# Two graph layers' aggregates as seven products of 128-column adjacency sums, with VectorE adding plus terms from PSUM

## The chip, the cores and the metric

The kernel runs on one core of one Trainium2 chip. The metric is the device time of one execution in microseconds (us). The core's engines are TensorE (PE, with its weight loads as PEld), VectorE (DVE), ScalarE (ACT), GpSimd (POOL) and SyncE (SP), which issues the transfers. Each engine has its own instruction queue and works through it in order; semaphores tie the queues together.

## The reference

There are 64 graphs of 256 nodes and 512 features, all in float32. Two layers follow each other:

```python
h = relu(adj @ (x @ W1) + b1)
h = relu(adj @ (h @ W2) + b2)
x = layernorm(x + adj @ (h @ W3) + b3)

q, k = split(x @ Wqk); v = x @ Wv
agg = adj @ (k * mask[:, :, None])
w = inv_scale * mask * sum(q * agg, axis=-1)
x = layernorm(x + softmax(w)[:, :, None] * v)
```

The inputs' mask is all ones, but the kernel applies it.

## The kernel before

Graphs are taken in 32 pairs (G = 2). All tiles have 128 partitions; 512 float columns fill one of the eight PSUM banks.

Most products use the same scheme, `seven`: a 2x2 block product made of seven block products instead of eight, from sums of the blocks of either operand. It runs the products in the order 1, 7, 6, 2, 5, 4, 3 in three PSUM banks, copies three partial results to SBUF tiles named `tmp` (ScalarE), and ends each of the four result blocks with a function that its caller gives (`c11`, `c12`, `c21`, `c22`). Where the caller gives `plus`, GpSimd adds that term to the copied tile.

For each pair of graphs:

- `support` (L304) computes h @ W with `seven`, once for each of the three layers. Its left operands are the blocks of the activations and their sums, made by `a_sums` (four sums, all on GpSimd); its right operands are weight blocks and sums made once.
- `aggregate` (L326) computes adj @ support for layers 1 and 2, without `seven`: four PSUM banks, one for each 128 output features, with two 256-column matmuls for each graph. ScalarE applies bias and ReLU out of PSUM into `hT` (L329), and GpSimd makes the next `a_sums`.
- `adj_times` (L362) computes adj @ something with `seven` and sums of adj (`adj_sums`, GpSimd) and of the other operand (`t_sums`, four sums on GpSimd): once for layer 3, once for the attention's gather of the normalized `xm`.
- `back` adds x, makes the statistics (BN_STATS, L439 and L441), `xm` on ScalarE (L456), the normalized `r` (L458) and its transposes (L484) on VectorE, which go through DRAM to become `x1T`.
- `attention` (L542) multiplies by W products held in DRAM as 28 slices, `mv`, read through a ring of seven SBUF tiles (`ring`): each use issues the fetch for the seventh use after it. It nests `seven` twice: 28 inner steps, of which the last 14 alternate between two matmuls and one.
- `finish` does softmax over the nodes, the last sum, layer norm and the store.

These parts are Python generators. Steps of F (`front`: supports and aggregates of one pair), S (`sums`), B (`back`) and G, M (gather and attention of the pair before), and E (`finish` of the pair before that) are interleaved by four strings written out by hand: START for the first pair, ORDER for most, LAST and END for the last ones. One letter runs one generator up to its next `yield`. The strings so fix the order of instructions on every engine.

Of the kernel before, what the change touches and what calls it, by code (L numbers as in the profile page):

```python
# [14 lines left out]
P = 128  # L15
# [5 lines left out]
def gcn_then_graph_attention(ctx: ExitStack, tc: tile.TileContext, xT, xN, adjT, mask, W1, b1, W2, b2, W3, b3,  # L21
                             WqT, WkT, Wv, out):

# [7 lines left out]
    KEYS = ("T1", "T2", "T3", "T4")  # L47

# [12 lines left out]
    def tmp():  # L61
        return pool.tile([P, D], FP, name="tmp", bufs=6)
# [3 lines left out]

    def padd(o, a, b, op=OP.add):
        nc.gpsimd.tensor_tensor(o, a, b, op=op)  # L68
# [18 lines left out]
    def load_x(i):  # L87
        t = pool.tile([P, G, NH, D], FP, name="x", tag="x", bufs=1)
        nc.sync.dma_start(t, xN[i].rearrange("p (g h f) -> p g h f", g=G, h=NH))
        return t  # L90


    def b_steps(B, Ts, eng):

        sub = OP.subtract
        for o, a, b in ((2, B[3], B[1]), (0, B[1], B[0]), (1, B[3], Ts[0]), (3, B[2], Ts[1])):
            eng.tensor_tensor(Ts[o], a, b, op=sub)
            yield

    def b_sums(B, Ts, eng):  # L100
        for _ in b_steps(B, Ts, eng):
            pass

    def shaped(shape):
        t = tmp()
        if len(shape) == 2:
            return t
        return t[:, :shape[1] * shape[2]].rearrange("p (a b) -> p a b", a=shape[1])

    def seven(mm, shape, c11, c12, c21, c22, plus=None):  # L110

        x = bank(shape)
        mm(1, x, True)
        t1 = shaped(shape)
        nc.scalar.copy(t1, x)  # L118
        if plus is not None:
            padd(t1, t1, plus[0])  # L120
        yield
        v = bank(shape)
        mm(7, v, True)
        yield
        mm(6, x, False)
        u = shaped(shape)
        nc.scalar.copy(u, x)  # L127
        yield
        y = bank(shape)
        mm(2, y, True)  # L130
        t7 = shaped(shape)
        nc.scalar.copy(t7, v)  # L132
        if plus is not None:
            padd(t7, t7, plus[2])
            padd(u, u, plus[1])
        c11(y, t1)
        yield
        mm(5, x, False)
        c22(x, t7)
        yield  # L140
        mm(4, v, False)
        c21(v, u)
        yield
        mm(3, x, False)
        c12(x)
        yield

# [44 lines left out]
    mask_t = const.tile([P, NH, NPAIR * G], FP, name="mask_t")  # L192
    mask_s = const.tile([P, NH, NPAIR * G], FP, name="mask_s")
    eps = const.tile([P, 1], FP, name="eps")
    nc.vector.memset(eps, EPS)

    def prepare():

        for n, w in ((2, W2), (3, W3)):
            begin, end = load_w(w, n)  # L200
            begin()
            yield from end()
        aTs[1] = load_adj(1)
        nc.sync.dma_start(b3b, b3.partition_broadcast(P))
        nc.sync.dma_start(mask_t, mask.rearrange("p (h b) -> p h b", h=NH))
        yield
        nc.vector.tensor_scalar(mask_s, mask_t, ISCALE, None, op0=OP.mult)
        yield from make_m()
# [66 lines left out]
    def a_sums(blk, eng=nc.gpsimd):  # L275

        S = [pool.tile([P, 2, G, P], FP, name="S", tag="S", bufs=8) for _ in range(4)]
        sub = OP.subtract  # L280

        def first():
            eng.tensor_tensor(S[2], blk(0, 0), blk(1, 0), op=sub)  # L283

        def rest():
            eng.tensor_tensor(S[0], blk(1, 0), blk(1, 1), op=OP.add)  # L286
            eng.tensor_tensor(S[1], S[0], blk(0, 0), op=sub)  # L287

        def last():
            eng.tensor_tensor(S[3], blk(0, 1), S[1], op=sub)  # L290
        return {1: blk(0, 0), 2: blk(0, 1), 4: blk(1, 1), 5: S[0], 6: S[1], 7: S[2], 3: S[3]}, first, rest, last

# [4 lines left out]
    def support(src, w, last=None):  # L297

        C = [[pool.tile([P, G, HD], FP, name="sup", tag="sup", bufs=7) for _ in range(2)] for _ in range(2)]

        def mm(n, ps, first):
            for g in range(G):
                for c in range(2):
# [3 lines left out]
        steps = seven(mm, (P, G, HD), lambda y, t: add(C[0][0], y, t), lambda x: nc.scalar.copy(C[0][1], x),  # L307
                      lambda v, t: add(C[1][0], v, t), lambda v, t: add(C[1][1], v, t))
# [7 lines left out]

    def aggregate(C, aT, b):


        hT = [pool.tile([P, 2, G, N], FP, name="hT", tag="act", bufs=2) for _ in range(2)]  # L320
        src, first, rest, last = a_sums(blocks(hT))
        for c in range(DC):
            ps = bank()
            for g in range(G):
                for k in range(NH):
                    nc.tensor.matmul(ps[:, g], lhsT=C[k][c // 2][:, g, (c % 2) * P:(c % 2 + 1) * P],  # L326
                                     rhs=aT[:, k, g], start=(g == 0 and k == 0), stop=(g == G - 1 and k == NH - 1),
                                     skip_group_check=True)
            nc.scalar.activation(hT[c // 2][:, c % 2], ps, AF.Relu, bias=b[:, c:c + 1])  # L329
            if c == 1:  # L330
                first()
            if c == 3:
                rest()
            yield
        return src, last

    def adj_sums(aT, put):
        S = pool.tile([P, 4, G, P], FP, name="aS", bufs=1)
        blk = lambda i, k: aT[:, k, :, i * P:(i + 1) * P]
        sub = OP.subtract  # L340
        padd(S[:, 0], blk(1, 0), blk(1, 1))
        yield
        padd(S[:, 1], S[:, 0], blk(0, 0), sub)
        yield
        padd(S[:, 2], blk(0, 0), blk(1, 0), sub)
        yield
        padd(S[:, 3], blk(0, 1), S[:, 1], sub)
        put["aS"] = {1: blk(0, 0), 2: blk(0, 1), 4: blk(1, 1), 5: S[:, 0], 6: S[:, 1], 7: S[:, 2], 3: S[:, 3]}

    def t_sums(B):  # L350
        T = pool.tile([P, 4, G, HD], FP, name="T", tag="T", bufs=1)
        Ts = [T[:, k] for k in range(4)]
        b_sums((B[0][0], B[0][1], B[1][0], B[1][1]), Ts, nc.gpsimd)
        return Ts

    def adj_times(aS, B, Ts, c11, c12, c21, c22, plus=None):

        mov = {1: B[0][0], 2: B[1][0], 3: B[1][1], 4: Ts[3], 5: Ts[0], 6: Ts[1], 7: Ts[2]}
# [17 lines left out]
    def softmax_rows(w, gs):  # L376
# [7 lines left out]
        e = small.tile([n, N], FP, name="e", bufs=1)  # L384
# [5 lines left out]
        return e  # L390

    def softmax_cols(sm, gs):
        n = len(gs)
        ps = bank((P, NH, n))
        for h in range(NH):
            nc.tensor.transpose(ps[:, h, :], sm[:, h * P:(h + 1) * P], ident[:n, :n])  # L396
# [5 lines left out]
    def front(i, hT, src, aT, put):  # L402
        C = yield from support(src, wl[1])
        if i + 1 < NPAIR:
            put["xT"] = load_xT(i + 1)
        src, last = yield from aggregate(C, aT, bcol[0])
        C = yield from support(src, wl[2], last)
        src, last = yield from aggregate(C, aT, bcol[1])
        put["x"] = load_x(i)
        return (yield from support(src, wl[3], last))  # L410

    def sums(i, aT, put):

        fs = [lambda: None] * 3
        if i + 1 < NPAIR:
            put["S"], *fs = a_sums(blocks(put["xT"], True))
# [4 lines left out]
        for g in range(G):  # L421
            for h in range(NH):
                padd(x[:, g, h, :], x[:, g, h, :], b3b)
                yield
        yield from adj_sums(aT, put)

    def back(i, C, aS, x, end, put):
        Ts = t_sums(C)
# [13 lines left out]
        yield from adj_times(aS, C, Ts, lambda y, t: add(rb(0, 0), y, t), lambda x: block(rb(0, 1), x, xb(0, 1), 0),  # L442
# [5 lines left out]
        b = i * G  # L448
        mrs = small.tile([P, NH, G], FP, name="mrs")
        nc.vector.tensor_tensor(mrs, rs, mask_t[:, :, b:b + G], op=OP.mult)  # L450
        mnb = small.tile([P, NH, G], FP, name="mnb")
        nc.vector.tensor_tensor(mnb, nb, mask_t[:, :, b:b + G], op=OP.mult)
# [9 lines left out]
        if end:  # L462
# [6 lines left out]
            Ts = t_sums(xmb)  # L469
# [7 lines left out]
        else:  # L477
# [15 lines left out]
            Ts = t_sums(xmb)  # L493
# [4 lines left out]
        def gather():  # L498
            steps = adj_times(aS, xmb, Ts, lambda y, t: add(gb(0, 0), y, t), lambda x: nc.scalar.copy(gb(0, 1), x),
# [9 lines left out]
        put["M"] = attention(i, x1b, w, r, put)  # L509

    def attention(i, x1b, w, r, put):
# [42 lines left out]
        flat = lambda R: R.rearrange("p g j f -> p g (j f)")  # L554

        def score(R, h, g):
            t = put["gt"][:, h, g, :]
            b = i * G + g
            nc.vector.scalar_tensor_tensor(t, R[:, g].rearrange("p j f -> p (j f)"), mask_s[:, h, b:b + 1], t,  # L559
                                           op0=OP.mult, op1=OP.mult, accum_out=w[:, h, g:g + 1])  # L560

        def results(g):
# [6 lines left out]
            put[g] = r, v, w  # L569
# [21 lines left out]
    def finish(i, prev, gs=range(G)):  # L591
# [3 lines left out]
        sm = softmax_rows(w, gs)  # L595
        yield
        s = softmax_cols(sm, gs)
# [16 lines left out]
        for k, g in enumerate(gs):  # L614
            for h in range(NH):
# [5 lines left out]


    ORDER = ("BFEFFFEBFBEFBBBFBBFBBFFFBFBESBEFBBGFFGEFEEGEGFFEFESFFGMMGSFEMGMMFMMMMMMMMMMMMMMMMMFM"
             "MMMMMSFMMMSSMMSMSSFMFSMFMMEMSMMFM")
    START = ("FBBFBFFFBBFBBBFBBFBBBBFBFFBBBBBBFBBFBBBBBBBBFFFFBBFBBBBBBFFBBSBFFBFBBSFBBBFFSBBBFSBB"
             "BBSBFBSBFBSSSSBSBBBSBBB")
    LAST = ("BFEFFFEBFBEFBBBFBBFBBFFFBFBESBEFBBGFFGEFEEGEGFFEFESFFGMMGSFEMGMMFMMMMMMMMMMMMMMMMMFM"
            "MMMMMSFMMMSSMMSMSSFMFSMFMMEMSMMFM")
    END = ("EEBEBEBEEBBBEEEBBBEEBBBBBBGMGMGBGMMBMEMMMMMGGMMMBMMMMGMMMMMMMMMMMMMMMMMMXMXMMMMXMMYM"
           "XMXXMXMYMYYYXXYYMMXXMYXYYYY")  # L630
# [16 lines left out]
    xS, *fs = a_sums(blocks(xTs, True))  # L647
    for f in fs:
        f()
    for i in range(NPAIR + 1):  # L650
        gens, put, done = {}, {}, {}
        if i < NPAIR:
            gens["F"] = front(i, xTs, xS, aTs[i], put)
            gens["S"] = sums(i, aTs[i], put)
# [18 lines left out]
        if i < NPAIR:  # L673
            state = (res["F"], put["aS"], put["x"])
            xTs, xS = put.get("xT"), put.get("S")
# [35 lines left out]
```

## Time and profile before

| | |
|---|---|
| Median of 3 runs | 2777.42 us (2775.81 to 2778.24) |
| Profiled execution, span (the page has no other time of it) | 2778.9 us |
| Granted TensorE clock, mean | 0.994 of full speed |
| Transfers | 403 MB, mean 145 GB/s |
| Idle time of L542's matmuls before `ring` landed | 13.1 us |

A line of the profile names an engine, an operation, the tiles that it writes and reads, how often it ran, and its durations. "Idle before" is the time that the engine was not busy just before such an instruction, with what ended it. TensorE's records: a float32 matmul leaves two.

### The profile page before, as it was taken

What the parts mean: (1) busy time and instruction counts of PE and PEld (TensorE: products, weight loads), DVE (VectorE), ACT (ScalarE), POOL (GpSimd) and SP (SyncE); (2) the same over time, 40 slices, a digit from 0 to 9 for tenths busy, and PEclk for the clock granted to TensorE, in tenths of its full rate; (3) what the DMA queues carried; (4) which work ended last, traced back from release to release, by engine and by line L of the source; (5) the groups of instructions that cost most, each with busy time, mean ns of one, the idle gap of its engine ahead of it and who ended that gap; (6) DMA issues with size and microseconds to landing.
All of it is one profiled execution on the core that took longest, in us unless ns stands there. A gap on an engine that the chain in (4) does not pass through costs nothing.

```text
span 2778.9 us, 37024 instructions
## 1 busy us (share of the span) xinstructions
PE 2731.4 (98%) x12688; PEld 2377.9 (86%) x12688; DVE 1723.4 (62%) x2900; ACT 1143.7 (41%) x1890; POOL 1795.9 (65%) x1446
## 2 busy tenths in 40 slices
PE   9999999999999999999999999999999999999996
PEld 8888888888888888888888888888888888888875
DVE  4566565665566665656666666655566655666666
ACT  3334344434444433444334444334443334443434
POOL 3666765676756666656667666767566676667663
PEclk9999999999999999999999999999999999999997
DMA  6444554344554345543445543455444455434442
GB/s 223 153 122 131 163 174 136 113 146 150 162 166 130 118 139 169 161 148 125 134 139 161 171 134 116 139 161 161 154 126 127 139 161 173 137 112 145 139 153 97
DMA packets 197752, 403.45 MB, mean 145 GB/s; under 512 B 20160, under 2 KB 57408, under 8 KB 189504
## 3 DMA queue, kind: packets, MB, share of 16 engines
q1 hardware_dynamic: 197568, 401.10, 45.8%
q8 instruction: 103, 1.69, 0.3%
q14 instruction: 81, 0.66, 0.1%
HBM read 328.54 MB, written 72.48 MB: 144 GB/s over the span
## 4 chain that ended last, share of the span: by engine, by line
PE 93%; DMA 3%; DVE 2%; issue 1%; POOL 1%; ACT 0%; SPq 0%; POOLq 0%; ACTq 0%; DVEq 0%
PE ps L304 41%; PE ps L542 22%; PE ps L326 16%; PE ps L362 14%; DMA ring<-mv 3%; PE ps L246 1%; DVE v L600 0%; DVE gt L559 0%; PE ps L381 0%; PE ps L396 0%; DMA xT<-in_xT 0%; DVE R L65 0%; POOL S L286 0%; POOL tmp L68 0%; DVE st L607 0%
## 5 line engine op out<-in xcount | busy, mean ns | idle before, releaser
L304 PE MATMUL ps<-w_T,S 128*128 128x256 f32 x2304 | 539.7, 379 | 3.8 <-POOL S L287 2.8
L304 PEld LDWEIGHTS ps<-w_T,S 128*128 128x128 f32 x2304 | 435.1, 190 | 63.9 <-POOL S L287 4.0
L326 PE MATMUL ps<-aT,sup 128*128 128x256 f32 x2048 | 457.7, 379 | 0.0
L65 DVE TENSOR_TENSOR R<-ps,tmp 128x512 f32<-128x512 f32 (+1 forms) x384 | 230.5, 622 | 365.5 <-PE ps L542 350.3
L542 PE MATMUL ps<-ring,I 128*128 128x256 f32 x1792 | 428.5, 381 | 13.3 <-DMA ring<-mv 13.1
L326 PEld LDWEIGHTS ps<-aT,sup 128*128 128x128 f32 x2048 | 389.0, 190 | 52.8
L283 POOL TENSOR_TENSOR S<-hT 128x512 f32<-128x512 f32 x64 | 81.7, 1277 | 492.1 <-ACT hT L329 492.1
L542 PEld LDWEIGHTS ps<-ring,I 128*128 128x128 f32 x1792 | 339.7, 190 | 64.7 <-issue 15.1
L127 ACT COPY tmp<-ps 128x512 f32<-128x512 f32 (+1 forms) x288 | 158.0, 560 | 446.7 <-PE ps L542 183.8
L65 DVE TENSOR_TENSOR sup<-ps,tmp 128x512 f32<-128x512 f32 x288 | 197.4, 686 | 211.6 <-PE ps L304 211.6
L542 PE MATMUL ps<-ring,Z 128*128 128x256 f32 x1344 | 321.6, 379 | 0.0
L68 POOL TENSOR_TENSOR tmp<-tmp,R 128x512 f32<-128x512 f32 (+1 forms) x192 | 213.1, 1137 | 160.2 <-DVE R L579 141.2
L542 PEld LDWEIGHTS ps<-ring,Z 128*128 128x128 f32 x1344 | 255.4, 190 | 34.7
L307 ACT COPY sup<-ps 128x512 f32<-128x512 f32 x96 | 56.2, 585 | 457.1 <-PE ps L304 303.6
L68 POOL TENSOR_TENSOR I<-Z 128x384 f32<-128x384 f32 (+1 forms) x128 | 177.7, 1409 | 100.6 <-DVE Z L523 97.1
L304 PE MATMUL ps<-w,hT 128*128 128x256 f32 x1024 | 241.9, 379 | 0.0
L118 ACT COPY tmp<-ps 128x512 f32<-128x512 f32 (+1 forms) x288 | 158.8, 563 | 172.1 <-PE ps L304 86.0
L304 PEld LDWEIGHTS ps<-w,hT 128*128 128x128 f32 x1024 | 194.6, 190 | 26.4
L329 ACT ACTIVATE hT<-ps,b 128x512 f32<-128x512 f32 x256 | 171.3, 681 | 98.6 <-PE ps L326 96.9
L68 POOL TENSOR_TENSOR tmp<-tmp,x 128x512 f32<-128x512 f32 x96 | 120.5, 1270 | 128.7 <-ACT tmp L132 128.4
L65 DVE TENSOR_TENSOR gt<-ps,tmp 128x512 f32<-128x512 f32 x96 | 65.4, 682 | 222.6 <-PE ps L362 222.6
L68 POOL TENSOR_TENSOR x<-x,b3b 128x512 f32<-128x512 f32 x128 | 202.3, 1600 | 0.0
(111 smaller groups left out, 4755.0 us busy)
## 6 DMA issues: line engine op xcount, KB each, us to landing
ring<-mv SPq DMA_DIRECT2D x672, 256.0 KB, 3.5
x<-in_xN SPq DMA_DIRECT2D x32, 1024.0 KB, 6.0
out<-v SPq DMA_DIRECT2D x64, 512.0 KB, 2.7
xT<-in_xT SPq DMA_DIRECT2D x31, 1024.0 KB, 4.8
via<-tr SPq DMA_DIRECT2D x31, 1024.0 KB, 4.3
x1T<-via SPq DMA_DIRECT2D x124, 256.0 KB, 4.7
ring<-mv SPq DMA_DIRECT2D x224, 128.0 KB, 2.9
aT<-in_adjT SPq DMA_DIRECT2D x32, 512.0 KB, 3.5
```

The lines of the kernel that those rows point to most:

```text
L65: nc.vector.tensor_tensor(o, a, b, op=OP.add)
L68: nc.gpsimd.tensor_tensor(o, a, b, op=op)
L118: nc.scalar.copy(t1, x)
L127: nc.scalar.copy(u, x)
L246: nc.tensor.matmul(pt[:, j * P:(j + 1) * P], lhsT=wq[:, d, f * P:(f + 1) * P], rhs=wk[:, d, j * P:(j + 1) * P], start=(d == 0 and j == 0), ...
L283: eng.tensor_tensor(S[2], blk(0, 0), blk(1, 0), op=sub)
L304: nc.tensor.matmul(ps[:, g], lhsT=src[n][:, c, g], rhs=w[n][:, c], start=(first and g == 0 and c == 0), stop=(g == G - 1 and c == 1), skip ...
L307: steps = seven(mm, (P, G, HD), lambda y, t: add(C[0][0], y, t), lambda x: nc.scalar.copy(C[0][1], x), lambda v, t: add(C[1][0], v, t), la ...
L326: nc.tensor.matmul(ps[:, g], lhsT=C[k][c // 2][:, g, (c % 2) * P:(c % 2 + 1) * P], rhs=aT[:, k, g], start=(g == 0 and k == 0), stop=(g == ...
L329: nc.scalar.activation(hT[c // 2][:, c % 2], ps, AF.Relu, bias=b[:, c:c + 1])
L362: nc.tensor.matmul(ps[:, g], lhsT=aS[n][:, g], rhs=mov[n][:, g], start=(first and g == 0), stop=(g == G - 1), skip_group_check=True)
L542: nc.tensor.matmul(ps[:, k], lhsT=left[n](place[o]), rhs=wt[:, k], start=(first and k == 0), stop=(k == len(outer) - 1), skip_group_check= ...
```

## The change

The aggregates of layers 1 and 2 use `seven` too. Their right operands are the 128-column blocks of adj and their three sums, which `adj_sums` now makes one pair ahead (one sum is written in place). Their left operands are blocks of the support and sums of them: `support` makes these in its last step, two from PSUM on VectorE and two by `unit`. The result blocks are added into `hT`, and ScalarE applies bias and ReLU in place, in two calls a block.

`seven` no longer copies by ScalarE where a plus term is given: VectorE adds the term straight from PSUM into `tmp`. Layer 3's `t_sums` is gone, as the support has the sums. `a_sums` and `adj_sums` write one of their sums in place, so that they need three tiles. A list, ON_DVE, says which sums VectorE makes; the others stay on GpSimd. The mask is loaded for each pair, and its scale is applied in `back`; the softmax tile is allocated once, and its transposes became plain matmuls. All four order strings are new; M, B, E, G and S have as many steps as before in each, and F has 35 in place of 29.

```diff
+    ON_DVE = ('a3', 'a5', 'a6', 'a7', 'c1T6', 'c2T4', 'c2T6', 'h13', 'h15', 'h16', 'h25', 'h26', 'h27', 'x3', 'x5', 'x6', 'x7')
+    def unit(name, o, a, b, op=OP.add):
+        (nc.vector if name in ON_DVE else nc.gpsimd).tensor_tensor(o, a, b, op=op)
 def seven(mm, shape, c11, c12, c21, c22, plus=None):
+        def out(ps, k):
+            t = shaped(shape)
+            if plus is None:
+                nc.scalar.copy(t, ps)
+            else:
+                add(t, ps, plus[k])
+            return t
-        t1 = shaped(shape)
-        nc.scalar.copy(t1, x)
-        if plus is not None:
-            padd(t1, t1, plus[0])
+        t1 = out(x, 0)
...
 def support(src, w, who, last=None):
-        C = [[pool.tile([P, G, HD], FP, name="sup", tag="sup", bufs=7) for _ in range(2)] for _ in range(2)]
+        sup = lambda: pool.tile([P, G, HD], FP, name="sup", tag="sup", bufs=SUP)
+        C = {k: sup() for k in (1, 3, 2, 5, 7)}
...
+        def c12(x):
+            sub(C[7], C[3], x)
+            sub(C[5], x, C[1])
+            C[6], C[4] = sup(), sup()
+            unit(who + "T6", C[6], C[3], C[5], OP.subtract)
+            unit(who + "T4", C[4], C[2], C[6], OP.subtract)
...
 def aggregate(C, aS, b, who):
-        for c in range(DC):
-            ps = bank()
-            for g in range(G):
-                for k in range(NH):
-                    nc.tensor.matmul(ps[:, g], lhsT=C[k][c // 2][:, g, (c % 2) * P:(c % 2 + 1) * P],
-                                     rhs=aT[:, k, g], start=(g == 0 and k == 0), stop=(g == G - 1 and k == NH - 1),
-            nc.scalar.activation(hT[c // 2][:, c % 2], ps, AF.Relu, bias=b[:, c:c + 1])
+        def relu(i, j, ps=None):
+            o = blk(i, j)
+            for c in range(2):
+                nc.scalar.activation(o[:, c], (o if ps is None else ps)[:, c], AF.Relu, bias=b[:, 2 * j + c:2 * j + c + 1])
+        def block(i, j, a, t):
+            add(blk(i, j), a, t)
+            relu(i, j)
+        def mm(n, ps, first):
+            for c in range(2):
+                for g in range(G):
+                    nc.tensor.matmul(ps[:, c, g], lhsT=C[n][:, g, c * P:(c + 1) * P], rhs=aS[n][:, g],
+                                     start=(first and c == 0 and g == 0), stop=(c == 1 and g == G - 1),
+        for k, _ in enumerate(seven(mm, (P, 2, G, P), lambda y, t: block(0, 0, y, t), lambda x: relu(0, 1, x),
+                                    lambda v, t: block(1, 0, v, t), lambda v, t: block(1, 1, v, t))):
+            if k == 5:
+                first()
+            if k == 6:
+                rest()
...
 def t_sums(B):
-        b_sums((B[0][0], B[0][1], B[1][0], B[1][1]), Ts, nc.gpsimd)
+        for n, o, a, b in (("x7", 2, B[3], B[1]), ("x5", 0, B[1], B[0]), ("x6", 1, B[3], Ts[0]), ("x4", 3, B[2], Ts[1])):
+            unit(n, Ts[o], a, b, OP.subtract)
...
 def back(i, C, aS, x, mask, end, put):
-        Ts = t_sums(C)
...
-    ORDER = ("BFEFFFEBFBEFBBBFBBFBBFFFBFBESBEFBBGFFGEFEEGEGFFEFESFFGMMGSFEMGMMFMMMMMMMMMMMMMMMMMFM"
-             "MMMMMSFMMMSSMMSMSSFMFSMFMMEMSMMFM")
+    ORDER = ("BBFFEFBFFEBFBFFBFFFFFBEFBFBBBFBFBBFBEGEFFGGGGFFMMGFGFMMMFFMFMMEMMSMEMMEEEFFMMESMSSEM"
+             "SFMFMFSMFFSMFMSMMMMMMEMMMSMSMSMMMMMMMMM")
...
```

## The prediction

> **What bounds the kernel now.** I read the busy line first, then the chain of work that ended last, to see whether another engine sets the pace.
>
> ```profile
> PE 2731.4 (98%) x12688; PEld 2377.9 (86%) x12688; DVE 1723.4 (62%) x2900; ACT 1143.7 (41%) x1890; POOL 1795.9 (65%) x1446
> PE 93%; DMA 3%; DVE 2%; issue 1%; POOL 1%; ACT 0%; SPq 0%; POOLq 0%; ACTq 0%; DVEq 0%
> PE ps L304 41%; PE ps L542 22%; PE ps L326 16%; PE ps L362 14%; DMA ring<-mv 3%; PE ps L246 1%; DVE v L600 0%; DVE gt L559 0%; PE ps L381 0%; PE ps L396 0%; DMA xT<-in_xT 0%; DVE R L65 0%; POOL S L286 0%; POOL tmp L68 0%; DVE st L607 0%
> ```
>
> TensorE is the bound: 47.5 us of the 2778.9 us span are not its work, and nothing else carries over 3% of the chain. Fewer matmul microseconds shorten the kernel as long as TensorE is fed. L326 is the part that the change rewrites. A pair takes 84.15 us from one softmax transpose to the next where no wait for the ring falls into it (mean of all about 84.7).
>
> Next, the critical chain in order of time, for the price of a matmul of either width (start, us, what, number of records; a float matmul leaves two records).
>
> ```profile
> 23.06 14.29 PE ps L246 x128
> 265.05 6.91 PE ps L326 x32
> ```
>
> L246 streams 128 columns, 111.6 ns a record, 0.2233 us a matmul. L326 streams 256, 215.9 ns a record, 0.4318 us a matmul. Both load a new 128x128 weight each time.
>
> Then single lines, with shortest, median and longest duration, for VectorE's prices.
>
> ```profile
> L65 DVE TENSOR_TENSOR sup<-ps,tmp x288: 673/690/693, 16.3 to 2700.1; 128x512 f32<-128x512 f32 x144
> L523 DVE TENSOR_TENSOR Z<-Z x64: 691/1226/1781, 125.2 to 2732.5; 128x512 f32<-128x512 f32 x64
> ```
>
> An addition from PSUM takes 0.69 us whatever else runs. One of two SBUF tiles takes 0.69 us as well, but up to 1.78 us while GpSimd works. Back to back they overlap by 0.085 us, so each holds VectorE 0.605 us, or 0.725 us if the next needs its result.
>
> Last, VectorE's timeline of one steady pair, where layer 3's sums end and the attention's input is normalized.
>
> ```profile
> 1028.07 0.69 DVE L65 TENSOR_TENSOR r<-ps,x 128x512 f32<-128x512 f32 x1 [0.26 <-PE ps L362]
> 1028.79 1.29 DVE L439 BATCH_NORM_STATS2 st<-r 128x6 f32<-128x512 f32 x2
> 1030.00 0.30 DVE L441 BATCH_NORM_AGGREGATE mvt<-st 128x2 f32<-128x6 f32 x2
> 1030.66 0.18 DVE L371 RECIPROCAL rs<-sd 128x4 f32<-128x4 f32 x1 [0.36 <-ACT sd L369]
> ...
> 1031.07 0.16 DVE L452 TENSOR_TENSOR mnb<-nb,mask_t 128x4 f32<-128x4 f32 x1
> 1032.44 0.55 DVE L458 TENSOR_SCALAR r<-r,rs,nb 128x512 f32<-128x512 f32 x1 [1.21 <-ACT xm L456]
> 1033.02 1.07 DVE L484 STREAM_TRANSPOSE tr<-r 128x256 f32<-128x256 f32 x2
> 1033.95 1.37 DVE L458 TENSOR_SCALAR r<-r,rs,nb 128x512 f32<-128x512 f32 x1
> ```
>
> This is the chain that I price below: today the T sums at its end are GpSimd's.
>
> **The aggregates.** A layer has 16 matmuls of 256 columns (6.91 us); after the change 28 of 128: 28 x 0.2233 = 6.25 us. That is 0.66 us a layer, 1.32 a pair, and over 64 layers **-42.1 us**, all on TensorE.
>
> A rule speaks against this. "TensorE: Matmul & The Clock Gate" in the Trainium skill, section "Back-to-back issue gap", gives 81 ns for a sustained matmul of 128 columns with its weight load and 131 ns for 512. A straight line between makes 256 columns about 98 ns, an estimate; 28 narrow ones would then cost 1.45 times the 16 wide ones, +6.2 us a pair or about +199 us in all. L246's row contradicts it for this data type, so I use the row.
>
> **VectorE's load.** From the instruction lists: 576 additions of 512 columns from PSUM come to VectorE (192 write hT, 192 make sup, 192 add plus terms), 96 of 256 columns, 512 of SBUF tiles of 512 columns, 128 of 256. At 0.605, 0.33, 0.66 and 0.34 us that is 348 + 32 + 338 + 44 = 762 us. GpSimd loses more than half its work (1796 to about 800 us), which lets VectorE's SBUF work go faster: the 128 score operations (L559) average 1.43 us against a shortest of about 0.74, so -80, and some -50 elsewhere. VectorE ends near 2350 us, 85%. It is no bound in total, but its queue is long, and its order decides when TensorE gets its operands. ScalarE has two shorter ReLU calls a block but loses the copies ahead of plus terms; it stays near 42%.
>
> **The new wait.** In the order after the change I looked for each product whose operand now comes from VectorE and counted TensorE's work before it. One hand-off comes short: the attention's gather (adj_times on xm). Its product 7 needs T's x7, made on VectorE behind everything in the timeline above and, by ON_DVE, behind layer 1's sums h15, h16 and h13 of the next pair (h17 stays on GpSimd). From the end of layer 3's last product, TensorE has until then: the aggregate's product 3 (4 x 0.2233), supports 1, 7, 6, 2 (16 x 0.4318), the gather's product 1 (0.86), supports 5 and 4 (3.45): **12.12 us**. VectorE meanwhile: 0.20 until r<-ps,x starts, 2.23 until the aggregates of statistics end (1028.07 to 1030.30), then new in between one st<-v (0.60 less 0.08 of overlap), h15 and h16 (0.725 + 0.605): 4.28. Reciprocal to mnb 0.57, ScalarE's xm 0.93 (the median gap there), four groups of L458 and two transposes at 1.51 without GpSimd (1032.44 to 1033.95): 11.82. h13 0.605, x7 0.69 and 0.04 to TensorE: **13.16 us**. TensorE waits 1.04 us. Product 6 needs x5 and x6, 1.33 us after x7, and has 0.86 of cover: 0.47 more. So 1.5 us a pair in 31 pairs, **+46 us**. It eats the whole saving. Behind the late x7 VectorE holds sup additions of support 2, 5 and 4; these have at least 3 us of cover. Bounds: 0.7 us a pair if gaps overlap better (+22), 2.2 if h15, h16 or L458 meet GpSimd (L458's second row shows 1.37 for 0.55; +68). I take 1.5: GpSimd's only sum there, h17 (1.27 us), should end before VectorE's SBUF work begins.
>
> **What is relieved.** Layer 3's T sums leave GpSimd's serial queue and are made with the support; of the 0.4 us that a pair is longer than its matmuls (193 x 0.4318 + 0.43 for the softmax), half lies at support 3's wait at the end of the pair, for its GpSimd sum: 0.2 x 31 = **-6** (0 to -6). The ring costs 13.1 us today, in 13 pairs, where the 1 MB load of x is queued on SP between fetches. After the change x, the small mask load (32 more issues) and the two output stores are issued where the next seven fetches have about 14 us before use. But support products no longer lie between the small ring products: six fetches a pair must land within 3.89 us of the use before (nine matmuls). They land in 3.5 us (256 KB) or 2.9 us (128 KB) in the median, plus 0.2 to issue. I take 0.3 us a pair, 9 instead of 13: **-4** (-13 to +15).
>
> **Ends.** Order END starts the last pair's layer 3 before the softmax, where TensorE now waits 2.1 and 3.5 us, and needs no GpSimd T sums: **-8** (-12 to 0). At the start VectorE makes the first x and adj sums beside weight sums: **+3** (0 to +7). The hoisted softmax buffer, mask scaling and wider tile counts move no wait that I can find: 0.
>
> **Sum** against the profiled span 2778.9 (median of the runs 2777.4, 1.5 less): -42 + 46 - 6 - 4 - 8 + 3 = **-11**, or 2768 of span, 2766 as a run. What a measurement of this kernel can tell is about 0.2%, 5.6 us.
>
> **Rivals.**
> *VectorE's chain is longer (slower).* One mechanism: the SBUF operations between the statistics and x7 collide with GpSimd, or VectorE enters the chain late because it is dense from the scores on. Each 0.1 us is 3 us. Above 1.9 us a pair the sign turns; at 2.7 it is +26, 2803. For: L458 and Z<-Z collide today. Against: GpSimd does less than half. Chance 0.24.
> *The ring becomes the bound.* 0.8 us a pair at the small products, 384 KB in 1.3 us or about 300 GB/s, above any slice of the page (223): +16 against my sum, 2782, about no change. Chance 0.12.
> *The hand-off is covered.* If x7 is at most 0.7 us late: 24 better, 2742. For: the pieces overlap by 0.08 to 0.15 us each, which I may undercount. Chance 0.14.
> *The narrow matmuls do not pay* (weight loads of 0.19 us bind): above 2820; L246 speaks against. Chance 0.02.
> *Forecast:* 0.48, 2750 to 2778.
>
> **Numbers.** The range reaches from the covered hand-off to the longer chain: 2740 to 2803. Faster by over 0.2%: 0.38 of the forecast, the covered case and some of the ring case, 0.58. Same: 0.15. Slower: 0.27.
>
> **What would show it.** The matmuls of the aggregates at 111 to 113 ns a record; VectorE near 85% and GpSimd near 30%; the wait of the gather's T products for VectorE's T at the top of TensorE's waits, about 1.0 and 0.5 us a pair; waits for the ring near 9 us; a pair of 84.3 us. I am wrong if that wait is missing or twice as long, if VectorE's sums of two SBUF tiles average over 0.9 us, or if another product waits in every pair.

## The result and the profile after

The changed kernel is slower: 2856.24 us in the median (2854.83 to 2861.6) against 2776.61 (2773.03 to 2778.24), a ratio of 1.0286 [1.0271, 1.0301], 80 us. The forecast was 2766, the range ended at 2803.

The busy line of the page after, and the groups of the two lines that matter (busy time and mean ns of a record; then the idle time before them and what ended most of it):

```profile
PE 2745.4 (96%) x14290; PEld 2403.9 (84%) x14290; DVE 2328.3 (81%) x4212; ACT 1096.2 (38%) x1954; POOL 775.1 (27%) x582
L543 PE MATMUL ps<-ring,Z 128*128 128x256 f32 x1344 | 345.9, 391 | 47.0 <-ACT Z L521 42.0
L328 PE MATMUL ps<-aT,sup 128*128 128x128 f32 x2048 | 258.6, 278 | 0.0
```

The load moved as forecast, GpSimd to VectorE. But the attention's first products now stand idle for ScalarE's `Z`, which ended no wait of TensorE before. The view of waits, after (total, times, longest):

```profile
ACT Z L521 <- DMA x1T<-via: 87.9, 31, 4.1
PE ps L543 <- ACT Z L521: 42.0, 61, 2.4
PE ps L364 <- DVE T L62: 18.4, 59, 0.4
PE ps L543 <- DMA ring<-mv: 6.7, 15, 1.2
```

ScalarE waits in every pair for `x1T`, the transposed input that comes back through DRAM; VectorE, which makes sums of `x1T` for `Z`, waits for it too (51.2 us in all). TensorE waits in every pair for `Z`, and, as predicted, for `T`. The ring is where it was put.

These idle times begin at modelled ends of matmuls. For a budget I used starts instead: the time from one matmul record to the next, less the usual pitch (216 ns for 256 columns, 112 for 128), put down to what released the later one. In microseconds:

| Lost on TensorE | before | after |
|---|---|---|
| First 165 (after: 180) us | 10.4 | 25.5 |
| Steady part | 26.6 | 134.3 |
| ... of it waiting for Z | 0 | 50.7 |
| ... for T | 0 | 27.6 |
| ... for the ring | 12.9 | 8.6 |
| Last 120 us or so | 28.1 | 22.9 |

The differences are +15.1, +107.7 and -5.2; with -42.1 for the narrower aggregates that is +75.5 of the 80.9 by which the spans differ. The other 5 us I can't place.

Where Z's wait comes from is seen in one pair's timeline. Before (start, length; the first row is layer 3's last product, then the trip to DRAM, its way back, the copy to `Z`, the first attention product):

```profile
1027.00 1.03 PE L362 MATMUL ps<-sup,aS 128*128 128x256 f32 x4
...
1039.86 0.37 SPq L488 DMA_DIRECT2D via<-tr  x1
...
1044.22 1.75 SPq L490 DMA_DIRECT2D x1T<-via  x4
...
1056.36 3.03 ACT L520 COPY Z<-x1T 128x512 f32<-128x512 f32 x3
...
1059.81 1.89 PE L542 MATMUL ps<-ring,Z 128*128 128x256 f32 x8
```

The same steps after:

```profile
1067.47 1.03 PE L364 MATMUL ps<-sup,aS 128*128 128x256 f32 x4
...
1079.82 0.66 DVE L62 TENSOR_TENSOR S<-hT,S 128x512 f32<-128x512 f32 x1
1079.98 0.37 SPq L489 DMA_DIRECT2D via<-tr  x1
1080.41 1.26 DVE L62 TENSOR_TENSOR T<-xm 128x512 f32<-128x512 f32 x2
...
1081.21 1.10 PE L364 MATMUL ps<-T,aS 128*128 128x256 f32 x4 [0.40 <-DVE T L62]
...
1084.27 2.10 SPq L491 DMA_DIRECT2D x1T<-via  x4
...
1091.62 3.00 ACT L521 COPY Z<-x1T 128x512 f32<-128x512 f32 x3 [2.94 <-DMA x1T<-via]
...
1092.73 0.70 PE L543 MATMUL ps<-ring,Z 128*128 128x256 f32 x2 [1.15 <-ACT Z L521]
1093.71 1.56 PE L543 MATMUL ps<-ring,Z 128*128 128x256 f32 x6 [0.28 <-ACT Z L521]
```

The trip itself is as long as before: 12.9 and 12.5 us from the product's start to the issue of `via`, then 4.4 and 4.3 us to the issue of `x1T`. Before, the copy to `Z` began 12.1 us after that issue and waited for nothing; after, 7.4 us, as soon as the data is there, and TensorE is already idle. Medians over all pairs, from the end of layer 3's last product to the first attention product ("to DRAM" ends where the way back is issued; medians need not add up):

| | normalize, transpose | to DRAM | back | spare before the Z copy | Z copy to product | sum |
|---|---|---|---|---|---|---|
| before | 12.0 | 4.4 | 6.8 | 5.3 | 3.5 | 31.9 |
| after | 11.6 | 4.3 | 6.9 | 0.1 | 1.1 | 24.1 |

Without any slack the trip takes about 24 us. Adding the usual pitches of the records in between, waits left out, gives TensorE's other work in the meantime: 32.0 us in the old order and 21.7 in the new one. The difference to 24.1 is, within 0.1 us, what it waits at T and Z (0.9 and 1.6 us a pair).

### The profile page after: what moved, and what is told of

Its sections match the earlier page's. It is cut to its first block, busy times and chain, and to the rows that moved or that the text cites. A ratio compares the mean times of both kernels' runs of the same rounds, so it can differ in the third digit from the quotient of the medians.

```text
span 2859.8 us, 40774 instructions
## 1 busy us (share of the span) xinstructions
PE 2745.4 (96%) x14290; PEld 2403.9 (84%) x14290; DVE 2328.3 (81%) x4212; ACT 1096.2 (38%) x1954; POOL 775.1 (27%) x582
## 5 line engine op out<-in xcount | busy, mean ns | idle before, releaser
L109 ACT COPY tmp<-ps 128x512 f32<-128x512 f32 x768 | 422.5, 585 | 1419.3 <-PE ps L290 581.8
L290 PE MATMUL ps<-w_T,S 128*128 128x256 f32 x1536 | 359.8, 382 | 4.1 <-DVE S L62 4.1
L290 PEld LDWEIGHTS ps<-w_T,S 128*128 128x128 f32 x1536 | 288.6, 191 | 52.0 <-issue 10.1
L328 PEld LDWEIGHTS ps<-aT,sup 128*128 128x128 f32 x2048 | 255.8, 194 | 7.2 <-ACT tmp L109 0.2
L328 PE MATMUL ps<-aT,sup 128*128 128x128 f32 x2048 | 258.6, 278 | 0.0
L290 PE MATMUL ps<-w_T,hT 128*128 128x256 f32 x1024 | 231.8, 380 | 0.2 <-ACT tmp L109 0.2
L290 PEld LDWEIGHTS ps<-w_T,hT 128*128 128x128 f32 x1024 | 194.8, 190 | 26.7 <-ACT tmp L109 0.6
L290 PEld LDWEIGHTS ps<-w,hT 128*128 128x128 f32 x1024 | 190.1, 191 | 22.9
L328 PEld LDWEIGHTS ps<-aS,sup 128*128 128x128 f32 x1536 | 198.0, 192 | 8.5 <-issue 0.4
L328 PE MATMUL ps<-aS,sup 128*128 128x128 f32 x1536 | 199.6, 277 | 0.3 <-DVE sup L62 0.3
L290 PE MATMUL ps<-w,S 128*128 128x256 f32 x768 | 182.7, 381 | 7.6 <-DVE sup L53 7.6
L319 ACT ACTIVATE hT<-hT,b 128x256 f32<-128x256 f32 x384 | 168.1, 498 | 47.5 <-DVE hT L53 39.1
```

Source lines behind the costliest of these rows:

```text
L109: nc.scalar.copy(t, ps)
L290: nc.tensor.matmul(ps[:, g], lhsT=src[n][:, c, g], rhs=w[n][:, c], start=(first and g == 0 and c == 0), stop=(g == G - 1 and c == 1), skip ...
L319: nc.scalar.activation(o[:, c], (o if ps is None else ps)[:, c], AF.Relu, bias=b[:, 2 * j + c:2 * j + c + 1])
L328: nc.tensor.matmul(ps[:, c, g], lhsT=C[n][:, g, c * P:(c + 1) * P], rhs=aS[n][:, g], start=(first and c == 0 and g == 0), stop=(c == 1 and ...
```

## The experiments

**Theory:** the new order of steps took TensorE's cover off the trip through DRAM; this wait is worth over 50 us. **Rivals:** VectorE is too full, whatever the order; the wait at T is the cost; the plus terms on VectorE are.

A ratio is the variant's time over that of the kernel before, run beside it; these runs of before had medians of 2775.7 to 2785.9 us, so an expectation in us is best compared by the ratio (1% is 28 us).

**1. Move the attention's first steps in the order.** Everything but the string ORDER is as after.

```diff
-    ORDER = ("...GFGFMMMFFMFMM..."          # after
+    ORDER = ("...GFGFMFFMMMFMM..."          # z_later
+    ORDER = ("...GFGMMMFFFMFMM..."          # z_earlier
```

Expected of z_later: 

> ORDER alone: the first two attention products of a pair come after two steps of layer 2's aggregate (1.79 us of TensorE) instead of before them; same work. Chain theory (from the end of layer 3 to the first attention product runs a fixed chain of 24.1 us through VectorE, the round trip of x1T by DRAM and ScalarE's Z, and TensorE has about 1.7 us less work than that): the waits for Z, 50.7 us in the steady part, fall below 8 us and the kernel takes 2806 to 2818 us. Rival (VectorE is simply too full, 81% busy): the wait moves to other operands of VectorE, 2845 to 2860 us.

Expected of z_earlier: 

> ORDER alone, the other way: the first two attention products and GpSimd's second half of I come one aggregate step (0.89 us) earlier than after the change; same work. Chain theory: the wait for Z grows by 0.89 us a pair in 30 pairs, 2879 to 2888 us. Rival (VectorE too full): no change within 0.3%, 2848 to 2864 us.

z_earlier: ratio 1.042 [1.0387, 1.0453]; Z's wait rose from 50.7 to 72.7 us, 22 of the 27 us expected, so the direction is right. As a ratio 1.037 to 1.040 was expected; records at half speed, described in the last section, came on top, 29 us in place of 7. z_later missed: 1.055 [1.0524, 1.0576]. Z's wait is gone, but not the time. z_later's timeline:

```profile
1117.92 1.06 PE L328 MATMUL ps<-aT,sup 128*128 128x128 f32 x8
1118.24 3.00 ACT L521 COPY Z<-x1T 128x512 f32<-128x512 f32 x3 [3.05 <-DMA x1T<-via]
...
1121.15 0.57 ACT L500 COPY gt<-ps 128x512 f32<-128x512 f32 x1
1121.63 1.05 ACT L109 COPY tmp<-ps 128x512 f32<-128x512 f32 x2
...
1122.26 2.08 PE L328 MATMUL ps<-aT,sup 128*128 128x128 f32 x8 [3.28 <-ACT tmp L109]
```

I had moved products on TensorE, but the copies to `Z` are issued by an earlier step and stayed where they were in ScalarE's queue. They wait there for `x1T`, and behind them wait the copies that the moved aggregate needs: L328 lost 97.2 us that way. The last row also took twice its time, of which more below.

**2. Give T more cover in the order.**

```diff
-    ORDER = ("...GEFFGGGGFFMMGFGFMMMFFMFMM..."   # after
+    ORDER = ("...GEFFFGGGGFMMGFGFMMMFFMFMM..."   # t_later
+    ORDER = ("...GEFFFGGGGFMMGFGFMFFFMMMMM..."   # both_later
```

Expected of t_later: 

> ORDER alone: support 3 of layer 2 (1.73 us of TensorE) comes ahead of the gather's product 7, which waits for T from VectorE; same work. Chain theory: the wait for T (27.6 us in the steady part) goes, but it lies inside the 24.1 us chain, so the wait for Z grows by as much: 2850 to 2862 us, no change. Rival (the two waits are separate, each costs its own): 2826 to 2836 us.

Expected of both_later: 

> ORDER alone: support 3 of layer 2 ahead of the gather's product 7, and the first attention products after three aggregate steps (2.68 us) instead of before them; same work. Chain theory: both waits go, 78 us less 5 that remain elsewhere, 2778 to 2792 us. If VectorE is too full: above 2830 us.

Both missed: 1.0545 [1.0524, 1.0566] and 1.0612 [1.0593, 1.063]. The waits at T and Z are gone in both, and support 3 waits 124 and 128 us for VectorE. By these numbers alone VectorE could simply be too full; experiments 3 and 4, with the same work on VectorE, decide that. t_later's timeline:

```profile
1108.69 1.25 DVE L62 TENSOR_TENSOR T<-xm 128x512 f32<-128x512 f32 x2
1109.98 0.69 DVE L62 TENSOR_TENSOR T<-xm,T 128x512 f32<-128x512 f32 x1
1110.59 0.68 DVE L53 TENSOR_TENSOR sup<-ps,tmp 128x512 f32<-128x512 f32 x1
...
1112.38 1.27 DVE L53 TENSOR_TENSOR sup<-ps,tmp 128x512 f32<-128x512 f32 x2
...
1113.11 2.92 PE L290 MATMUL ps<-w,S 128*128 128x256 f32 x8 [4.01 <-DVE sup L53]
```

The product that now comes first needs a PSUM bank which VectorE must empty (`sup<-ps,tmp`), and that addition stands behind the normalization and T in VectorE's queue. None of these four moves of products alone made the kernel faster.

**3. Take the trip out of Z's way.** The copies and sums for Z read `xm`, which is ready long before; the attention's left operand is then not the transposed r, so the result is not the kernel's. All instructions and transfers stay.

```diff
-            x1b = lambda h, k: x1T[:, :, h, k].rearrange("p n c g -> p c g n")
+            x1b = lambda h, k: xm[:, :, h, k * HD:(k + 1) * HD].rearrange("p g (c n) -> p c g n", c=2)
```

> After the change, with Z copied from xm in place of x1T: this leaves out the use of the transposed r (its transposes and transfers still run), so that no product waits for the round trip by DRAM; orders unchanged. Chain theory: the wait for Z goes (50.7 us, and about 12 us of restarts and half clock behind it), the wait for T stays near 27 us: 2790 to 2805 us. Rival (VectorE is too full, the wait for Z only shows it): the wait moves to other operands and the time stays above 2830 us.

Measured: 1.0072 [1.0056, 1.0088]. The order, T's wait (27.7 us) and the work on VectorE are those of after. The wait for Z is gone, support products wait 15 us for `sup<-ps,tmp` in place of 8, and 2.1% of the time has gone with it.

**4. Shorten the trip, with the computation whole.** The 1 MB through DRAM goes as four transfers into four tiles, so that each way back starts when its own quarter has landed.

```diff
-            via = dram.tile([4, P, D], FP, name="via")
-            nc.sync.dma_start(via.rearrange("q p e -> p q e"), tr.rearrange("p q j h k c g -> p q (j h k c g)"))
+            via = [dram.tile([P, D], FP, name=f"via{q}") for q in range(4)]
+            for q in range(4):
+                nc.sync.dma_start(via[q], tr[:, q].rearrange("p j h k c g -> p (j h k c g)"))
```

Expected of after with this edit, split_via: 

> After the change, with the round trip of x1T by DRAM cut in four: each quarter is written by a transfer of its own, and read back as soon as that quarter has landed. Same work and order otherwise, 3 more transfers a pair. Chain theory: the round trip (11.2 us from the first issue to the last landing) gets 2 to 3.5 us shorter, the wait for Z (1.7 us a pair) goes, the wait for T stays: 2790 to 2808 us. Rival (VectorE too full, products wait for it wherever they stand): above 2830 us.

Expected of before with this edit, before_split: 

> The kernel before the change with the same cut of the round trip in four. Before the change x1T had landed 5.3 us ahead of Z's first copy, so a shorter trip frees nothing. Chain theory: no change, 2768 to 2786 us. If the cut helps by itself (transfers, not the wait for Z): below 2760 us.

split_via: 1.002 [1.0011, 1.0029], so it takes back nearly the whole loss. before_split: 1.0007 [0.9998, 1.0016]: the same edit is worth nothing where the trip had 5.3 us to spare. That is the theory's signature. split_via's timeline:

```profile
1044.78 1.03 PE L364 MATMUL ps<-sup,aS 128*128 128x256 f32 x4
...
1057.31 1.79 SPq L490 DMA_DIRECT2D via<-tr  x4
...
1059.39 2.73 SPq L492 DMA_DIRECT2D x1T<-via  x4
...
1067.58 3.03 ACT L522 COPY Z<-x1T 128x512 f32<-128x512 f32 x3 [1.57 <-DMA x1T<-via]
...
1068.73 0.68 PE L544 MATMUL ps<-ring,Z 128*128 128x256 f32 x2
```

The first way back is issued 2.1 us after the first way out, not 4.3, and the first product has no wait ahead of it. Z's waits fall from 50.7 to 3.5 us.

**5. What the wait at T is worth.** First, all three of layer 1's sums that VectorE makes ahead of T go to GpSimd; then only h13, the one directly ahead of it, without and with the cut of experiment 4.

```diff
-    ON_DVE = (..., 'h13', 'h15', 'h16', 'h25', ...)
+    ON_DVE = (..., 'h25', ...)                    # h_pool
+    ON_DVE = (..., 'h15', 'h16', 'h25', ...)      # h13_pool; split_h13 with the cut
```

Expected of h_pool: 

> After the change, with layer 1's sums h13, h15 and h16 made by GpSimd as before the change instead of VectorE; order unchanged. Chain theory: 1.3 us less on VectorE before the last transpose and 1.9 us less before T's x7, so the waits for T (0.9 us a pair) and Z (1.7) fall to 0 to 0.2 and 0.4 to 0.8: 2800 to 2820 us, less what support 2's product 6 waits for GpSimd (up to 0.6 us a pair). Rival (GpSimd's sums collide with VectorE's SBUF work and lengthen it by as much): 2845 to 2870 us.

Expected of h13_pool: 

> After, with only h13 (layer 1's sum for product 3) on GpSimd; h15 and h16 stay on VectorE. In the changed kernel h13 takes 0.6 us of VectorE's time directly ahead of T. Theory (TensorE's waits for T lie inside the time that covers the transposed input's way through DRAM): T's waits fall by about 0.6 us a pair (27.6 to about 10 us) and Z's rise by as much (50.7 to about 68), so the time stays within 6 us of 2856. Rival (T's wait is a cost of its own): 2836 to 2844. If h13 on GpSimd collides with VectorE's normalization, the way to Z gets longer and it is slower than 2862.

Expected of split_h13: 

> The same move of h13, with the way through DRAM cut into four transfers, where Z has no wait to give back. Theory: T's waits fall from 27.6 to about 10 us and nothing takes their place, 2770 to 2780, faster than the kernel before by 0.2 to 0.6 per cent. Rival (GpSimd's h13 comes late for support 2's product 3, or its port delays VectorE's normalization, as when all three sums went to GpSimd): 2795 to 2830.

The theory's range missed each time: 1.044 [1.0411, 1.0469], 1.0478 [1.0434, 1.0522] and 1.0185 [1.0168, 1.0203]. What came for h13_pool and split_h13 is the other case that their texts name, a collision with VectorE's normalization. In h_pool T's wait is gone, Z's rose to 75.0, and a product of support 2 waits 22.4 us for GpSimd's sums. In h13_pool Z's wait rose to 73.5, more than T's fell (to 21.9). split_h13's timeline shows why:

```profile
1061.72 1.28 POOL L62 TENSOR_TENSOR S<-hT,S 128x512 f32<-128x512 f32 x1 [2.11 <-DVE rs L373]
1061.78 1.24 DVE L451 SCALAR_TENSOR_TENSOR mrs<-rs,mask 128x4 f32<-128x4 f32 x1
```

GpSimd's h13 starts 0.06 us before a VectorE operation of four columns, which takes 1.24 us, ending just after h13 does. Without that neighbour it is short; after:

```profile
1072.86 0.15 DVE L451 SCALAR_TENSOR_TENSOR mrs<-rs,mask 128x4 f32<-128x4 f32 x1
```

So moving 0.6 us off VectorE's chain put 1.1 us on it, ahead of the normalization and so of the whole trip. It is so in nearly every pair; of split_h13, with shortest, median and longest duration:

```profile
L451 DVE SCALAR_TENSOR_TENSOR mrs<-rs,mask x32: 155/1235/1239, 113.7 to 2770.1; 128x4 f32<-128x4 f32 x32
```

The Trainium skill, "SBUF — State Buffer", section "SBUF: two separate sides", says that a VectorE operation with two SBUF inputs and a GpSimd operation that reads SBUF exclude each other for a whole instruction; these rows agree, for a VectorE operation of only four columns.

So h13 was left on VectorE and only exchanged with T in its queue, which changes nothing on the other compute engines.

```diff
-        for _ in range(2):
+        for _ in range(3 if who == "c2" else 2):    # in support: when the caller's last sum is issued
             next(steps)
             yield
```

Expected of t_first, without the cut: 

> After, with VectorE's sum h13 behind the three T sums instead of directly ahead of them (it is still made by VectorE; nothing else changes place on TensorE, ScalarE or GpSimd). Theory: T's waits fall by up to 0.6 us a pair, from 27.6 to about 10 us; the way of the transposed input through DRAM does not change, and TensorE reaches the first Z product that much earlier, so Z's waits rise from 50.7 to about 68 and the time stays within 6 us of 2856. Rival (T's wait is a cost of its own): 2836 to 2844.

Expected of split_t_first, with it: 

> The same exchange of h13 and T, with the way through DRAM cut into four transfers. Theory: T's waits fall from 27.6 to about 10 us; Z's, 3.5 us with the cut, gives back at most 6, and h13 is still in time for support 2's product 3, so 2774 to 2782, within 0.3 per cent of the kernel before on either side. Rival (h13 comes late, or GpSimd's T sum makes it slow): 2790 to 2810.

t_first: 1.0305 [1.0276, 1.0334], the interval overlaps that of after. T's wait fell from 27.6 to 10.9 us, and TensorE's loss in the steady part is 134.3 us as it was: Z has 60.3 (+9.6), support products waiting for VectorE `sup<-ps,tmp` 11.2 (+3.6), and the attention's products that wait for R 5.7 (+3.8). So the time held, as the theory said, though Z took over 9.6 us and not all 17: the wait at T, which lies ahead of a longer wait, was worth nothing by itself. split_t_first missed its 0.3% with 1.0069 [1.0049, 1.009], inside the range of the other case: T fell to 10.9 here too, but Z went from 3.5 to 11.4, the support products from 6.8 to 9.6, and the ring from 2.3 to 12.2. A reading that fits: with the cut, Z is at the edge, and TensorE, earlier by 0.6 us, meets it again. That the ring's rise comes from the same shift was not tested.

**6. VectorE's load and the plus terms.** b_earlier issues layer 3's last product, which the statistics wait for, four F steps sooner. plus_pool undoes one part of the change: ScalarE copies and GpSimd adds the plus terms, as before.

```diff
-    ORDER = ("BBFFEFBFFEBFBFFBFFFFFBEF..."
+    ORDER = ("BBFFEFBFFEBFBFFBFBFFFFEF..."     # b_earlier
```
```diff
-            if plus is None:
-                nc.scalar.copy(t, ps)
-            else:
-                add(t, ps, plus[k])
+            nc.scalar.copy(t, ps)               # plus_pool
+            if plus is not None:
+                padd(t, t, plus[k])
```

Expected of b_earlier: 

> ORDER alone: layer 3's last product (B's seventh step) comes four steps of layer 1's aggregate (3.6 us of TensorE) earlier; same work. If the start of the chain is set by that product's place, both waits go: 2780 to 2795 us. If VectorE has no room ahead of the chain (it idles 0.4 us in the 14 us before it), the gain ends at 0.4 us a pair, and aggregate products wait for VectorE instead: 2840 to 2865 us.

Expected of plus_pool: 

> After the change, with plus terms as before it: ScalarE copies every partial result and GpSimd adds the term; order unchanged. Chain theory: these sums are not between the end of layer 3 and the attention, so the waits for T and Z stay: 2845 to 2862 us, or slower where GpSimd's later sums are waited for. Rival (VectorE's total of 81% is the bound): with about 170 us less on VectorE 2815 to 2835 us.

plus_pool: 1.0592 [1.0576, 1.0608]. VectorE is busy for only 75% of the span, yet the waits at T (26.2) and Z (46.4) stay and two others come: 57 us for `R` and 38 for the scores `gt`. Both are VectorE's; its line for `R` waits 89.6 us for GpSimd's `tmp`, the plus terms' sums. So the waits at T and Z need neither VectorE's total nor the plus terms on VectorE. b_earlier: 1.0411 [1.0388, 1.0434]. The trip was no sooner: from layer 3's last addition to the issue of `via` VectorE took 15.4 us in place of 11.4, since the work that was overtaken on TensorE now stands inside its queue (three additions into `hT`, and 2.1 us a pair of waiting for GpSimd's sum of the late `hT`). Products then waited for hT (25 us) and S (16 us).

**7. A faster version.** Starting from split_via, split_last issues the last sum of each `a_sums` after five support steps, in place of two; split_last_start also gives GpSimd the first pair's sums of xT and the sums of the attention's W slices.

```diff
-        for _ in range(2):
+        for _ in range(5):
```

Expected of split_last: 

> After the change, with the round trip cut in four and layer 1's (and 2's) last activation sum, h13, issued after five steps of the support instead of two, so that it stands behind T's sums on VectorE. Chain theory: the wait for Z is gone, and the wait for T falls from 0.9 us a pair to 0.3 or less: 2762 to 2785 us. If T's wait comes back at the last support product instead (it needs h13): 2790 to 2808 us, as with the cut alone.

Expected of split_last_start: 

> As the one before, and in the first pair the sums of xT and of the attention's W slices made by GpSimd, which is nearly idle there, instead of VectorE: of the 25 us that TensorE waits in the first 180 us, 6 to 12 should go: 2752 to 2777 us. If these waits are set by the loading of weights and by TensorE's own order: no change against the one before.

Both forecasts missed: 1.009 [1.0077, 1.0104] and 1.0106 [1.009, 1.0121]. T's wait fell to 10.9, but the sums so put off are late for their own products (12.6 us for GpSimd's, 8.4 for VectorE's in split_last), the second case that the text names. In split_last_start TensorE lost no less in the first 180 us (27 us, 24 in split_last). No version of the changed kernel that was tried beats the kernel before; the nearest is split_via, 0.2% slower.

## Why the prediction was wrong

**The step that failed** is the search for new waits: "I looked for each product whose operand now comes from VectorE and counted TensorE's work before it. One hand-off comes short." The list was made by who computes an operand. Z's makers did not change, so its product was never counted, though the change rewrote the order and with it the work ahead of every product. Counted in the same way, that hand-off had 21.7 us of cover for a trip of 24, all of whose pieces stood in the trace of before (12.0, 4.4, 6.8, and 1.1 for one copy to Z). The prediction had it at nothing. TensorE lost 50.7 us there by the starts; by the ratios of experiments 3 and 4 it cost 59 us (no_trip) to 74 (split_via, where the waits for the ring fell by 6 us as well) of the 80. It is the case the text named as its refutation: another product that waits in every pair.

**The aggregates** were right. In the timeline after, 24 records of 128 columns start at 1064.75 and the next product at 1067.47: 113 ns each. The two rows:

```profile
1064.75 2.89 PE L328 MATMUL ps<-aT,sup 128*128 128x128 f32 x24
...
1067.47 1.03 PE L364 MATMUL ps<-sup,aS 128*128 128x256 f32 x4
```

**VectorE's load** was right: 2328 us for 2350, GpSimd 775 for 800. With the same work on VectorE, no_trip and split_via take back most of the loss, so its total was not what bound.

**The wait at T** is where it was said to be, with 0.9 us a pair for 1.5. In the pair above, the product behind layer 3's last starts at 1068.34 and T's first product at 1081.21: 12.9 us for a computed 13.16, and TensorE had 12.3 us of work for a computed 12.12. More important, it was not a cost of its own: behind it lay the longer wait (t_first).

**Relieved:** the ring at 8.6 us for 9. The -6 for GpSimd's sums did not come: support 3's products (`ps<-w,S`) lost 6.1 us in the steady part before and 8.4 after, now mostly for VectorE's `sup<-ps,tmp`. **END** -5 for -8. **START** was a mis-sized term: +3 was given for VectorE's sums beside weight sums, and +15 measured. One wait makes about half of it, 7.0 us of the first pair's layer 3 for the support difference that VectorE makes behind weights' sums, which themselves waited 4.3 us for a transfer of weights (that wait was in no bound).

**The slower rival** had the sign but not the mechanism: no collision lengthens the chain to x7. VectorE's lines after, in which L458 is now L459 (shortest/median/longest):

```profile
L459 DVE TENSOR_SCALAR r<-r,rs,nb x128: 452/472/549, 116.5 to 2805.4; 128x512 f32<-128x512 f32 x128
L62 DVE TENSOR_TENSOR T<-xm x64: 656/671/687, 122.9 to 2806.5; 128x512 f32<-128x512 f32 x64
```

The ring did not become the bound, and the narrow matmuls paid.

## What to carry to other kernels

When a change rewrites the order of steps, recount the cover of every hand-off whose producer is not TensorE, the untouched ones first: begin with the longest trip in the old trace and ask how much of its cover was spare. An order is one schedule for all queues: a product moved on TensorE needs the copies and additions that empty its bank and make its operands to move with it. And before a wait is priced, look for a later one in the same stretch: removing the first only moves the time to the second.

## What the runs showed of the hardware

TensorE ran at half speed after long waits, which I had not priced. The granted clock from 1122.26 to 1126 us of z_later is 0.54; in after, from 1068 to 1072, it is 1.00. In z_later the eight 128-column records after a wait of 3.28 us took 2.08 us, in after the same number took 1.05 us; in t_later eight of 256 columns took 2.92 us after 4.01 us, in after 1.89. The rows of after:

```profile
1068.34 1.05 PE L328 MATMUL ps<-aS,sup 128*128 128x128 f32 x8
1069.23 1.89 PE L290 MATMUL ps<-w,hT 128*128 128x256 f32 x8
```

Records of 256 columns then start 427 ns apart in place of 216, those of 128 columns about 213 in place of 112, for a few us. Between 180 and 2750 us of after and its ten variants with the trip uncut, I counted the gaps between two records' starts behind which at least three of the next 24 records came at half speed: none of 116 gaps of 1 to 1.5 us, 24 of 100 up to 2 us, 15 of 47 up to 2.5, 22 of 27 up to 3, and 98 of 103 above 3. By the records that start at these longer pitches it cost about 7 us in after, 47 in z_later, 48 in t_later and 56 in both_later: in t_later, waits of about 4 us in every pair, 124 us in all, cost over a third more than themselves.

"TensorE: Matmul & The Clock Gate" in the Trainium skill, "Part 1: The HAM clock gate", has the clock halve after an idle window of about 3.4 us; the counts agree above 3 us, but gaps of 2 to 3 us had it in half of the cases too (37 of 74), and here the counts decide.

A four-column VectorE operation held up for 1.1 us by a GpSimd sum (experiment 5) was the other surprise: here an operation's size did not tell what a neighbour made it cost.
